# A fused graph-layer kernel: slot 5's one-hots moved behind block B's held sum, and block A transposed ahead of block B's second layer

## The chip, the cores and the metric

One core of one Trainium2 chip. The metric is the device time of one execution, in microseconds (us), and of several executions their median. Before the change it is 260.57 us (three runs, 260.36 to 260.77).

## What is computed

12500 nodes with 128 numbers each (`x`), 412500 edges with 48 numbers each (`edge_attr`), sorted by the node they point to (`dst`). The reference, cut to what matters:

```python
h = jnp.maximum(_layernorm(x, axis=-1), 0.0)
agg = jax.ops.segment_sum(edges, recv, num_segments=N_NODES)     # recv = dst
z = jnp.concatenate([h, agg, u], axis=1)      # u: the same 64 numbers for every node
out = x + (jax.nn.relu(z @ W1 + b1) @ W2 + b2)                   # hidden width 256
```

Everything is fp32. The edges are 79 MB of the 94 MB that are moved, the sum over edges most of the products.

## The kernel before, in words

**Staging.** The nodes are done in 12 turns of 1024; a turn has two blocks of 512, A (index 0) and B (index 1). The last 212 nodes (Z) come behind the loop. A turn's edges are 11 groups of 4 x 768 edges, kept in six slots: slots 0 to 3 and 5 hold two groups, slot 4 one. All tiles exist once; what overlaps is one turn's late part and the next one's early part.

**The sum over edges, as products.** For each slot VectorE compares an index with a row of numbers and so makes one-hots (`onehots`, tile `oh`, L745); TensorE multiplies edges by one-hots (`sums`, `su0` to `su5`, L801) into 28 sums per piece; ScalarE copies them to SBUF (`ss`, L805); a second product with one-hots of places (`pl`, made by VectorE at L751) adds them into two banks of 512 nodes, `ax` for A and `ay` for B (`place`, L823). What overlaps at the turn's ends goes through `pln` and `plf` (L785, `pc5`); the `pln` products read slot 5's copy.

**The nodes.** A and B are loaded from ScalarE's queue (`load_x`, L597), VectorE takes their statistics (`stats`, `stab`, L831) and from these `scab` and `shab`, ScalarE normalizes (`norm`, `xna` and `xnb`, L857), TensorE transposes (`turn`, `tu0` for A and `tu1` for B, L866), ScalarE copies the transposed blocks (`hta`, `htb`, L867). The first layer is two products per half of the hidden width, one from `hta` or `htb` (L876), one from the edge sums `ags` (L881); ScalarE applies bias and relu (L886). The second layer (`w20` for A, L907; for B `w21a`, 12 products at L901, and `w21`, 4 products at L907) is done in the next turn. VectorE adds its result to x + b2 in a held tile (`holda`, `holdb`, L911), and then overwrites `xba` or `xbb` by the next x + b2 (`add_b`, L861). When `xbb` is made, x of B is free and ScalarE issues the next load of B. All held tiles are stored at the end.

**What sets the order.** `body` lists the operations of a turn by hand, once for all engines. Each engine gets those of its own, in that order, as its queue; `Flow.order` works out the semaphores. An engine does its queue strictly in turn, so that a wait holds back all that stands behind it. VectorE, ScalarE, SP and GpSimd run a loop over the turns.

TensorE has a loop of its own (`Flow.run`): its turn is cut at an operation named by `f.mark`. What stands from there on (block "second") is placed at the loop's head, the rest ("first") behind it, so that a pass does the late part of one turn and the early part of the next. Operations named in `f.brief` are passed over in the first pass, where there is no second layer of an earlier turn: a compare on the register `turn` chooses between a block that only increments semaphores ("brief") and one that does the products ("whole"), and both come together in a block "both".

SP issues the loads of edges slot by slot as soon as TensorE has used them; the last in a turn is `le5.1`, slot 5's second group.

Of the kernel before, what the change touches and what calls it, by code (L numbers as in the profile page):

```python
# [28 lines left out]
R = 4  # L29
# [25 lines left out]
class Flow:  # L55
# [14 lines left out]
    def op(self, eng, name, reads, writes, emit, dma=False, late=None):  # L70
        self.seq.append(dict(eng=eng, name=name, r=tuple(reads), w=tuple(writes), emit=emit, dma=dma, it=self.at, late=late or {}))
# [119 lines left out]
    def run(self):  # L191
# [22 lines left out]
        def ahead(e, late=False):  # L214
            for n, c in sorted(self.ahead[e].items()):
                if (e == "PE" and n in self.weights) == late:
                    self.of[e].wait_ge(self.sem[n], (self.rank[n, c] + self.extra[n]) * self.unit(n))

        def repeat(o, i):
            waits = []  # L220
            for n, back in self.body.get(o["name"], []):
                u = self.unit(n)
                waits.append((n, self.sem[n], regs[(o["eng"], u, (self.at_lo[n] - lo - back + self.extra[n]) * u)]))
            self.emit(o, waits, i)
# [26 lines left out]
        pe = nc.tensor  # L251
        blocks = {}

        def part(name, over, come=True):

            if come:
                pe.br("pe_" + name)
            blocks[name] = nc.switch_bb("pe_" + name, parent=over and blocks[over])

        def either(under, yes, no):  # L260

            pe.br_lt(j, under, on_true="pe_" + yes, on_false="pe_" + no)

        n = 4
# [35 lines left out]
        at = "first"  # L300
        for brief, some in groupby(own[:cut], lambda o: o["name"] in self.brief):
            some = list(some)
            if not brief:
                for o in some:
                    if o["name"] in self.stops:
                        stop = "at_" + o["name"]
                        at = "go_" + o["name"]
                        above, under, to = over[stop]
                        part(stop, above)
                        either(under, to, at)  # L310
                        part(at, stop, False)
                    repeat(o, None)
                continue
            either(n + 1, "brief", "whole")
            part("brief", at, False)
            ahead("PE", True)
            for o in some:
                if o["name"] in self.sem:
                    pe.sem_inc(self.sem[o["name"]], 1)
            pe.br("pe_both")  # L320
            part("whole", at, False)
            for o in some:
                repeat(o, None)
            part("both", at)
        pe.br("pe_head")
        part("after", "gate2", False)
        self.straight(end)
# [151 lines left out]
def kernel(  # L479
# [37 lines left out]
    def bank(name):  # L517
        return psum.tile([P, BN], F32, name=name)
# [4 lines left out]
    ph = [bank("ph0"), bank("ph1")]  # L523
# [66 lines left out]
    f = Flow(nc, tc)  # L590
    op = f.op
    A, B, Z = 0, 1, 2

    def dma(eng, name, reads, writes, dst_ap, src_ap):
        def emit(i):
            with nc.allow_non_contiguous_dma(reason="small pieces"):
                return [f.of[eng].dma_start(dst_ap(i) if callable(dst_ap) else dst_ap, src_ap(i) if callable(src_ap) else src_ap)]  # L597
        op(eng, name, reads, writes, emit, dma=True)
# [31 lines left out]
    def rows_of(ap, i, a, m, r):  # L630
        return span(ap, i, a, m * r).rearrange("(p r) d -> p (r d)", r=r)

    def load_x(k, a, m=P, eng="ACT"):
        r = RR[k]
        dv = xt[k].rearrange("p r d -> p (r d)")
        q = m - m % 16
        dma(eng, f"lx{k}", [], [f"x{k}"], dv[:q], lambda i: rows_of(x, i, a, q, r))
        if q < m:
            dma(eng, f"lx{k}t", [], [f"x{k}t"], dv[q:m], lambda i: rows_of(x, i, lambda i: a(i) + q * r, m - q, r))
# [101 lines left out]
    def onehot(name, o, reads, r):  # L741

        k, n = r.shape[1], r.shape[2]
        ov = o.rearrange("p (k n) v -> p k n v", k=k)
        op("DVE", f"oh{name}", reads + ["iota_v"], [f"oh{name}"], lambda i: [nc.vector.tensor_tensor(  # L745
            ov, iota_v[:, None, None, :].to_broadcast([P, k, n, V]), r[:, :, :, None].to_broadcast([P, k, n, V]), OP.is_equal)])
# [6 lines left out]
    def onehots(s):  # L753
        g = SLOTS[s]
        onehot(s, oh[s], ["rel_i"], rel_i[:, g[0] - 1:g[0]] if len(g) == 1 else rel_i[:, g[0] - 1:g[1]:g[1] - g[0]])

    def split(name, o, some, reads, value):

        emits, c = [], 0
        for j, frm, w, _, _ in some:  # L760
            emits.append((c, j, frm, w))
            c += w
        op("DVE", name, reads + ["iota_w"], [name], lambda i: [
            nc.vector.tensor_scalar(o[:, c:c + w], iota_w[:, frm:frm + w], value(j), None, OP.is_equal) for c, j, frm, w in emits])
# [4 lines left out]
    def places_far():  # L769
        split("plf", plf, far_, ["off_i"], lambda j: off_i[:, SLOTS[-1][j] - 1:SLOTS[-1][j]])  # L770
# [17 lines left out]
    def keep_ends():  # L788
        op("ACT", "ssf", ["ss5"], ["ssf"], lambda i: [nc.scalar.copy(ssf, ss[5])])
# [17 lines left out]
    def sums(s):  # L807
        m = len(SLOTS[s])
        add_up(s, s % 2, oh[s], e[s], ss[s], [f"e{s}.{j}" for j in range(m)], m * CG, {1: (10, 36), 2: (36,)}.get(s, ()))
# [53 lines left out]
    def turn(k, m=P, bk=None, key="PT", eng="ACT"):  # L863
        pv = (pt if bk is None else bk)[:, :RR[k] * P].rearrange("p (r c) -> p r c", r=RR[k])
        copy = nc.scalar.copy if eng == "ACT" else nc.vector.tensor_copy
        op("PE", f"tu{k}", [f"xn{k}", "ident"], [key], lambda i: [nc.tensor.transpose(pv[:, r, :m], xn[k][:m, r], ident[:m, :m]) for r in range(RR[k])])  # L866
        op(eng, f"hT{k}", [key], [f"hT{k}"], lambda i: [copy(hT[k][:, :, :m], pv[:, :, :m])])  # L867

    def sums_out(k, m=P):
        h, r = HI * (k % 2), RR[k]  # L870
        op("ACT", f"ag{k}", [f"bk{k % 2}"], [f"ag{k}"], lambda i: [
            nc.scalar.copy(ag[k // 2][h:h + DE, :, :m], agg[k % 2][h:h + DE, :m * r].rearrange("p (c r) -> p r c", r=r))])
# [25 lines left out]
    def second_begun(k, bk, key, n):  # L898
        ov = bk.rearrange("p (r d) -> p r d", r=R)
        op("PE", f"w2{k}a", [f"hid{k}.{a}" for a in range(NH)] + ["w2"], [key], lambda i: [  # L900
            nc.tensor.matmul(ov[:, r], hid[k][:, a, r], w2[:, a], start=(a == 0), stop=(a == NH - 1)) for r in range(n) for a in range(NH)])  # L901
# [101 lines left out]
    def body(it):  # L1003
        f.at = it

        def add_slots(*some):
            for s in some:
                sums(s)
                if it < NIT - 1:
                    load_e(s, 1)  # L1010

        keep = lambda i: (i + NIT - 2) % (NIT - 1)
        add_slots(0, 1)
        stats(A)
        farthest()
        fetch(1)
        add_slots(2)
        stats(B)
        variance(0, (A, B))
        root(0)  # L1020
        onehots(0)
        add_slots(3)
        shift(0)
        norm(A, (0,))
        add_slots(4)
        norm(A, (1, 2))
        onehots(1)
        add_slots(5)
        norm(A, (3,))
        norm(B, range(R))  # L1030
        onehots(2)
        onehots(3)
        place(0, (0, 1))
        for s in (1, 2, 3, 4):
            place(s)
        place_ends((0, 1))
        second(A, P, ph[A], "PH0", keep)
        add_b(A)
        for s in (4, 5):
            onehots(s)  # L1040
        second_begun(B, ph[B], "PH1", R - 1)
        sums_out(A)
        sums_out(B)
        if it < NIT - 1:
            load_x(A, lambda i: (i + 1) % NIT * IN)
        turn(A)
        turn(B, P, po, "PO")
        second(B, P, ph[B], "PH1", keep, R - 1)
        add_b(B)
        keep_ends()  # L1050
        if it < NIT - 1:
            load_x(B, lambda i: (i + 1) % NIT * IN + BN)
        places_far()
        fetch_off(1)
        for s in (0, 1, 2, 3, 4):
            places(s)
        places_near()
        layers(layer_x)
        layers(layer_e)
        layers(relu)  # L1060
# [48 lines left out]
    for it in range(NIT):  # L1109
        body(it)  # L1110
# [1 line left out]
    f.at = NIT + 1  # L1112
    ends = [f"ot{k}" for k in range(3)] + [f"x{k}" for k in (A, B)] + [f"hold{k}.{j}" for k in (A, B) for j in range(NIT - 1)]
    op("SP", "end", [], ends, lambda i: [nc.sync.nop(nofuse=True)])
    f.mark, f.half, f.stops = "tu0", "of2", ("su1.b", "su1.c", "su2.b")
    f.brief, f.weights = ("w20", "w21a"), ("lw1h", "lw1a", "lw1b", "lw2")
    f.order((0, NIT - 1))
    tc.mark_branch_hint_location("skip", engines=[ET.PE, ET.DVE])
# [35 lines left out]
```

## Time and profile before

| | |
|---|---|
| median of 3 runs | 260.57 us (260.36 to 260.77) |
| the profiled execution | 260.67 us |
| its span, first to last instruction | 258.9 us |
| mean granted TensorE clock over the span | 0.965 |
| share of the span: TensorE, VectorE, ScalarE | 92%, 89%, 49% |
| moved by DMA | 94.33 MB, 364 GB/s over the span |
| longest waits of VectorE: for the load of B, 11 times | 6.9 us in sum, 0.8 at most |
| ScalarE's wait for A's transposes, 11 times | 12.2 us in sum, 2.1 at most |
| SP's wait for TensorE to free a slot, 11 times | 46.8 us in sum, 4.9 at most |

Times in the views are us from the start of the span, in one profiled execution. PE is TensorE, PEld its loading of weights, DVE VectorE, ACT ScalarE; `x4` counts instructions, and an fp32 product of the program is two of them. What stands in square brackets is the idle time of the engine ahead of the row and what ended it. A matmul's end is modelled, so that TensorE looks busy where it is not at its peak; a hole there is seen by the starts.

### The profile page before, as it was taken

The page shows a single profiled execution, that of the slowest core. Times are in us where ns is not written, and L with a number is a line of the kernel's source. Part 1 is how long each engine was busy: PE and PEld are TensorE (multiplying, and loading weights), DVE is VectorE, ACT ScalarE, POOL GpSimd, SP SyncE. Part 2 cuts the span into 40 slices and gives each one's busy share as a digit, 9 for nine tenths or more (in the row PEclk, how much of TensorE's full clock was granted, in tenths as well). Part 3 has the DMA queues.
Part 4 walks back from the last instruction along what each step waited for, and adds up shares of the span by engine and source line. Part 5 has one row for each costly group of instructions (what it writes and reads, how often), then busy time and mean ns, then how long its engine had stood idle before and what let it go on. Part 6 is the DMA issues. An engine that isn't in the chain of part 4 may idle for free.

```text
span 258.9 us, 17101 instructions
## 1 busy us (share of the span) xinstructions
PE 238.8 (92%) x7539; PEld 188.7 (73%) x7540; DVE 230.8 (89%) x572; ACT 127.9 (49%) x315; POOL 5.2 (2%) x18
## 2 busy tenths in 40 slices
PE   1866699899999999999999999999999999999990
PEld 1766565885976968949949869779589499598680
DVE  6699998978998998998998989989989989989740
ACT  5510273553644725725835646447257358355520
POOL 5000000000000000000000000000000000002000
PEclk9967579999999999999999999999999999999999
DMA  6999999999999999999999999999999999969951
GB/s 189 339 385 388 364 387 392 390 390 393 377 392 389 389 392 387 390 392 384 390 394 385 390 393 386 392 386 385 391 383 390 391 389 390 394 230 363 366 208 65
DMA packets 79508, 94.33 MB, mean 364 GB/s; under 512 B 3227, under 2 KB 72797, under 8 KB 79494
## 3 DMA queue, kind: packets, MB, share of 16 engines
q1 hardware_dynamic: 76086, 88.06, 95.5%
q10 hardware_dynamic: 3312, 6.03, 6.1%
q8 instruction: 7, 0.11, 0.2%
q0 software_dynamic: 96, 0.07, 0.1%
q14 instruction: 7, 0.06, 0.1%
HBM read 87.75 MB, written 6.40 MB: 364 GB/s over the span
## 4 chain that ended last, share of the span: by engine, by line
PE 78%; SPq 14%; DMA 4%; issue 1%; DVE 0%
PE s L801 23%; SPq L597 14%; PE ph L907 12%; PE ph L876 7%; PE ax L823 6%; PE ph L901 6%; PE pt L881 4%; PE pt L876 4%; DMA e<-in_edge_attr_dram 4%; PE ph L881 4%; PE po L876 4%; PE pt L866 2%; PE po L866 2%; PE ax L785 1%; PE ay L785 1%
## 5 line engine op out<-in xcount | busy, mean ns | idle before, releaser
L745 DVE TENSOR_TENSOR oh<-iota_v,rel_i 128x1344 f32<-128x1344 f32 (+1 forms) x78 | 108.7, 1435 | 0.0
L801 PEld LDWEIGHTS s<-e,oh 128*28 128x28 f32 x6336 | 74.2, 111 | 16.8 <-issue 14.5
L801 PE MATMUL s<-e,oh 128*28 128x48 f32 x6336 | 76.9, 212 | 7.4 <-issue 3.5
L886 ACT ACTIVATE hida<-pt,bias 128x512 f32<-128x512 f32 x12 | 8.2, 687 | 50.2 <-PE pt L881 50.2
L857 ACT ACTIVATE xna<-xa,shab,scab 128x128 f32<-128x128 f32 x48 | 23.7, 493 | 13.0 <-DVE shab L851 12.6
L805 ACT COPY ss<-s 128x96 f32<-128x96 f32 (+1 forms) x72 | 16.5, 229 | 26.5 <-PE s L801 25.7
L751 DVE TENSOR_SCALAR pl<-iota_w,off_i 128x186 f32<-128x186 f32 x117 | 27.6, 311 | 0.4
L907 PE MATMUL ph<-w,hida 128*128 128x128 f32 x192 | 24.6, 281 | 0.0
L857 ACT ACTIVATE xnb<-xb,shab,scab 128x128 f32<-128x128 f32 x48 | 23.5, 490 | 1.2
L907 PEld LDWEIGHTS ph<-w,hida 128*128 128x128 f32 x192 | 22.3, 191 | 0.6
L823 PE MATMUL ay<-pl,ss 128*48 128x186 f32 (+1 forms) x120 | 20.9, 324 | 0.0
L823 PE MATMUL ax<-pl,ss 128*48 128x186 f32 (+1 forms) x120 | 20.9, 324 | 0.0
L823 PEld LDWEIGHTS ax<-pl,ss 128*48 128x48 f32 x120 | 14.5, 129 | 4.1
L831 DVE BATCH_NORM_STATS2 stab<-xb 128x6 f32<-128x128 f32 x48 | 10.5, 282 | 6.9 <-DMA xb<-in_x_dram 6.9
L901 PE MATMUL ph<-w,hidb 128*128 128x128 f32 x132 | 16.5, 275 | 0.0
L901 PEld LDWEIGHTS ph<-w,hidb 128*128 128x128 f32 x132 | 15.6, 192 | 0.0
L823 PEld LDWEIGHTS ay<-pl,ss 128*48 128x48 f32 x120 | 14.5, 129 | 0.0
L876 PE MATMUL pt<-hta,w1h 128*128 128x512 f32 x24 | 13.5, 643 | 0.4 <-ACT hta L867 0.4
L881 PE MATMUL po<-ags,w1a 48*128 48x512 f32 x24 | 13.5, 641 | 0.0
L881 PE MATMUL pt<-ags,w1a 48*128 48x512 f32 x24 | 13.5, 641 | 0.0
L867 ACT COPY hta<-pt 128x512 f32<-128x512 f32 x12 | 7.0, 586 | 12.2 <-PE pt L866 12.2
L881 PE MATMUL ph<-ags,w1a 48*128 48x512 f32 x48 | 12.3, 589 | 0.0
(151 smaller groups left out, 330.3 us busy)
## 6 DMA issues: line engine op xcount, KB each, us to landing
e<-in_edge_attr_dram SPq DMA_DIRECT2D x133, 576.0 KB, 8.7
xa<-in_x_dram ACTq DMA_DIRECT2D x11, 256.0 KB, 5.4
xb<-in_x_dram ACTq DMA_DIRECT2D x11, 256.0 KB, 5.4
out_dram<-holda SPq DMA_DIRECT2D x11, 256.0 KB, 3.1
out_dram<-holdb SPq DMA_DIRECT2D x11, 256.0 KB, 3.1
holda<-in_dst_dram SPq DMA_DIRECT2D x4, 384.0 KB, 5.6
e<-in_edge_attr_dram SPq DMA_DIRECT2D x1, 720.0 KB, 4.7
xa<-in_x_dram SPq DMA_DIRECT2D x1, 256.0 KB, 6.6
```

What stands on the lines that cost most here:

```text
L597: return [f.of[eng].dma_start(dst_ap(i) if callable(dst_ap) else dst_ap, src_ap(i) if callable(src_ap) else src_ap)]
L745: op("DVE", f"oh{name}", reads + ["iota_v"], [f"oh{name}"], lambda i: [nc.vector.tensor_tensor(ov, iota_v[:, None, None, :].to_broadcast([ ...
L751: nc.vector.tensor_scalar(out[:, j], iota_w, o[j], None, OP.is_equal) for j in range(len(o))])
L801: nc.tensor.matmul(S[k][NV * c:NV * c + V, j * DE:(j + 1) * DE], o[:, (j * CG + c) * T + t], ev[:, j * CG + c, t * DE:(t + 1) * DE], start ...
L805: op("ACT", f"ss{name}", [f"S{k}"], [f"ss{name}"], lambda i: [nc.scalar.copy(sv.rearrange("p j d -> p (j d)"), S[k][:, :m * DE])])
L823: out.append(nc.tensor.matmul(agg[bk][h:h + DE, at:at + w], sv[:, j], pv[:, j, frm:frm + w], start=bk in fresh and bk not in seen, stop=Tr ...
L831: op("DVE", f"st{k}", [f"x{k}", f"x{k}t"], [f"st{k}"], lambda i: [nc.vector.bn_stats(st[k // 2][:m, c + r], xt[k][:m, r]) for r in range(R ...
L857: nc.scalar.activation(xn[k][:m, r], xt[k][:m, r], AF.Relu, bias=sh[n][:m, c + r:c + r + 1], scale=sc[n][:m, c + r:c + r + 1])])
L876: nc.tensor.matmul(o, w1h[:, a * P:(a + 1) * P], hT[k][:, :, :m], start=first, stop=False, skip_group_check=True)])
L881: nc.tensor.matmul(o, w1a[h:h + DE, a * P:(a + 1) * P], ag[k // 2][h:h + DE, :, :m], start=False, stop=True, skip_group_check=True)])
L901: nc.tensor.matmul(ov[:, r], hid[k][:, a, r], w2[:, a], start=(a == 0), stop=(a == NH - 1)) for r in range(n) for a in range(NH)])
L907: nc.tensor.matmul(ov[:m, r], hid[k][:, a, r, :m], w2[:, a], start=(a == 0), stop=(a == NH - 1)) for r in range(begun, RR[k]) for a in ran ...
```

## The change

Three things are moved in `body`. Slot 5's one-hots go from behind slot 4's to behind B's held sum and addition (`second(B, ...)`, `add_b(B)`, `keep_ends()`). Block A's transposes and their copy (`turn(A)`) go from behind the issue of A's load to ahead of it, and ahead of B's second layer (`second_begun`); the copies of the edge sums (`sums_out`) now stand ahead of both. To allow this, TensorE's turn is cut at `tu1` instead of `tu0`, and `w20` and `w21a`, which were one group with one choice between "brief" and "whole", become two groups with a choice each, since `tu0` stands between them.

```diff
@@ Flow.run
-            either(n + 1, "brief", "whole")
-            part("brief", at, False)
-            ahead("PE", True)
+            tag = some[0]["name"]
+            either(n + 1, "brief_" + tag, "whole_" + tag)
+            part("brief_" + tag, at, False)
+            if tag == self.brief[0]:
+                ahead("PE", True)
             for o in some:
                 if o["name"] in self.sem:
                     pe.sem_inc(self.sem[o["name"]], 1)
-            pe.br("pe_both")
-            part("whole", at, False)
+            pe.br("pe_both_" + tag)
+            part("whole_" + tag, at, False)
             for o in some:
                 repeat(o, None)
-            part("both", at)
+            part("both_" + tag, at)
+            at = "both_" + tag
@@ body
-        for s in (4, 5):
-            onehots(s)
-        second_begun(B, ph[B], "PH1", R - 1)
+        onehots(4)
         sums_out(A)
         sums_out(B)
+        turn(A)
+        second_begun(B, ph[B], "PH1", R - 1)
         if it < NIT - 1:
             load_x(A, lambda i: (i + 1) % NIT * IN)
-        turn(A)
         turn(B, P, po, "PO")
         second(B, P, ph[B], "PH1", keep, R - 1)
         add_b(B)
         keep_ends()
         if it < NIT - 1:
             load_x(B, lambda i: (i + 1) % NIT * IN + BN)
+        onehots(5)
         places_far()
@@ the names
-    f.mark, f.half, f.stops = "tu0", "of2", ("su1.b", "su1.c", "su2.b")
+    f.mark, f.half, f.stops = "tu1", "of2", ("su1.b", "su1.c", "su2.b")
```

VectorE's queue in the late part of a turn, before. `oh_91` and `oh_92` are the one-hots of slots 4 and 5, `holda` and `holdb` the held tiles, `plf` the first places of the next turn:

```order
L911 TENSOR_TENSOR holda<-ph_70,xba 128x512
L861 TENSOR_TENSOR xba<-xa,b_sb 128x512
L745 TENSOR_TENSOR oh_91<-iota_v,rel_i 128x672
L745 TENSOR_TENSOR oh_92<-iota_v,rel_i 128x1344
L911 REGISTER_ALU
L911 TENSOR_TENSOR holdb<-ph_71,xbb 128x512
L861 TENSOR_TENSOR xbb<-xb,b_sb 128x512
L764 TENSOR_SCALAR plf<-iota_w,off_i 128x46
```

And after (the lines are three higher in the changed file):

```order
L914 TENSOR_TENSOR holda<-ph_70,xba 128x512
L864 TENSOR_TENSOR xba<-xa,b_sb 128x512
L748 TENSOR_TENSOR oh_91<-iota_v,rel_i 128x672
L914 REGISTER_ALU
L914 TENSOR_TENSOR holdb<-ph_71,xbb 128x512
L864 TENSOR_TENSOR xbb<-xb,b_sb 128x512
L748 TENSOR_TENSOR oh_92<-iota_v,rel_i 128x1344
L767 TENSOR_SCALAR plf<-iota_w,off_i 128x46
```

`oh_92` has moved behind `holdb` and `xbb`; nothing else changes on VectorE.

TensorE's program at the end of the loop's body, before. `w20` is the row with `hida`, `w21a` the one with `hidb`; L262 and L320 are the compare and the end of "brief", L257 the jump behind "whole". A's transposes stand in the block at the loop's head, behind L269:

```order
L785 MATMUL ay<-pln,ss_106 48x46
L262 COMPARE_AND_BRANCH
L320 UNCONDITIONAL_BRANCH
L907 MATMUL ph_70<-w_141,hida 128x128 x8
L901 MATMUL ph_71<-w_141,hidb 128x128 x6
L257 UNCONDITIONAL_BRANCH
```

And after:

```order
L788 MATMUL ay<-pln,ss_106 48x46
L262 COMPARE_AND_BRANCH
L322 UNCONDITIONAL_BRANCH
L910 MATMUL ph_70<-w_141,hida 128x128 x8
L257 UNCONDITIONAL_BRANCH
L869 MATMUL pt<-ident,xna 128x128 x4
L262 COMPARE_AND_BRANCH
L322 UNCONDITIONAL_BRANCH
L904 MATMUL ph_71<-w_141,hidb 128x128 x6
L257 UNCONDITIONAL_BRANCH
```

A's transposes (`pt<-ident,xna`) stand between `w20` and `w21a`, with a jump and a compare more; the block at the loop's head begins with B's transposes (`po<-ident,xnb`). On ScalarE the copy of A (`hta<-pt`) stands behind the copies of the edge sums and ahead of the issue of A's load, where it stood behind it.

## The prediction

> **What bounds the kernel now.** I read the page first, for the share of each engine, then the table of stretches for one turn of the loop, then the chain of waits over all turns, then the timelines of VectorE, ScalarE and TensorE around the change, and last the landing times of the edge loads. The page's first part:
>
> ```profile
> PE 238.8 (92%) x7539; PEld 188.7 (73%) x7540; DVE 230.8 (89%) x572; ACT 127.9 (49%) x315; POOL 5.2 (2%) x18
> ```
>
> TensorE and VectorE are both nearly full, so the average does not decide. One turn in the table of stretches (PE, PEld, DVE, ACT, POOL, clock, DMA share, GB/s):
>
> ```profile
> 116.40:134.50 18.10, 18.10 (x614) 14.19 (x612) 17.17 (x43) 9.87 (x26) 0.00 (x0) 1.00 1.08 389
> ```
>
> TensorE looks full, VectorE has 0.9 us left, and the DMA engines move 389 GB/s at a share of 1.08: three candidates within a few per cent. The chain of waits (start, us, what) gives the pace. L907 hida x16 is block A's second layer, `w20`:
>
> ```profile
> 39.59 10.01 DMA e<-in_edge_attr_dram
> 49.65 0.71 PE s L801 x48
> 52.24 1.98 PE ph L907 x16
> ...
> 70.39 1.98 PE ph L907 x16
> ...
> 129.18 0.99 PE pt L876 x2
> 130.17 0.86 PE po L876 x2
> ...
> 232.90 1.98 PE ph L907 x16
> ...
> 237.54 0.92 PE pt L876 x2
> ```
>
> From 70.39 to 232.90 are nine turns: 162.51 / 9 = 18.06 us each. At 49.60 the kernel is held by an edge load, the last of its turn (`le5.1`, slot 5's second group); `w20` follows 2.64 us later. The same load one turn later and in the last turn, by SP's timeline and its time to landing:
>
> ```profile
> 57.70 1.35 SPq L597 DMA_DIRECT2D e<-in_edge_attr_dram  x1
> ```
>
> ```profile
> DMA to landing us min/median/max: 9.8/9.8/9.8
> ```
>
> ```profile
> 219.07 1.35 SPq L597 DMA_DIRECT2D e<-in_edge_attr_dram  x1
> ```
>
> ```profile
> DMA to landing us min/median/max: 10.0/10.0/10.0
> ```
>
> Landings at 67.50 and 229.07: 161.57 / 9 = 17.95 us a turn. The loads run 0.11 us a turn faster than the compute; from landing to `w20` it is 2.64, then 2.89, and 3.83 us in the last turn. So the DMA is not what sets 18.06, but it is only 0.11 us below. What does set it, on VectorE:
>
> ```profile
> 107.04 1.55 DVE L745 TENSOR_TENSOR oh<-iota_v,rel_i 128x1344 f32<-128x1344 f32 x1
> 108.51 0.68 DVE L911 TENSOR_TENSOR holda<-ph,xba 128x512 f32 x1
> 109.23 0.69 DVE L861 TENSOR_TENSOR xba<-xa,b_sb 128x512 f32<-128x512 f32 x1
> 109.84 2.32 DVE L745 TENSOR_TENSOR oh<-iota_v,rel_i 128x672 f32<-128x672 f32 x2
> 112.08 0.68 DVE L911 TENSOR_TENSOR holdb<-ph,xbb 128x512 f32 x1
> 112.80 0.69 DVE L861 TENSOR_TENSOR xbb<-xb,b_sb 128x512 f32<-128x512 f32 x1
> ...
> 116.48 0.87 DVE L831 BATCH_NORM_STATS2 stab<-xa 128x6 f32<-128x128 f32 x4
> ...
> 118.90 0.29 DVE L831 BATCH_NORM_STATS2 stab<-xb 128x6 f32<-128x128 f32 x1 [0.62 <-DMA xb<-in_x_dram]
> ```
>
> ScalarE issues block B's load once `xbb` is done (rows of ScalarE's timeline, and the load's time to landing):
>
> ```profile
> 109.95 0.41 ACTq L597 DMA_DIRECT2D xa<-in_x_dram  x1
> 110.40 0.59 ACT L867 COPY hta<-pt 128x512 f32<-128x512 f32 x1 [1.08 <-PE pt L866]
> ...
> 113.52 0.34 ACTq L597 DMA_DIRECT2D xb<-in_x_dram  x1
> ```
>
> ```profile
> DMA to landing us min/median/max: 5.4/5.4/5.4
> ```
>
> This is a closed ring: `xbb` ends at 113.49, the load of B is issued at 113.52 and lands 5.4 us later, `stab<-xb` starts at 118.90, VectorE then has no other wait until the next `xbb`. Period: 113.49 - 100.83 (the last turn's 118.90 - 18.07) = 12.66 of VectorE, plus 5.4, is 18.06, exactly the pace. The only idle time of VectorE in a turn, 0.62 us, lies in this ring. TensorE hangs on it through `shab` and ScalarE's queue:
>
> ```profile
> 122.29 0.49 ACT L857 ACTIVATE xna<-xa,shab,scab 128x128 f32<-128x128 f32 x1 [1.05 <-DVE shab L851]
> ...
> 122.82 1.02 ACT L857 ACTIVATE xna<-xa,shab,scab 128x128 f32<-128x128 f32 x2
> 123.74 0.22 ACT L805 COPY ss<-s 128x96 f32<-128x96 f32 x1
> ```
>
> ```profile
> 123.82 0.24 PE L823 MATMUL ax<-pl,ss 128*48 128x93 f32 x1
> 123.83 0.24 PE L823 MATMUL ay<-pl,ss 128*48 128x93 f32 x1
> 123.90 0.28 PE L785 MATMUL ax<-plf,ssf 128*48 128x140 f32 x1
> 124.02 0.32 PE L785 MATMUL ay<-pln,ss 128*48 128x140 f32 x1
> ```
>
> Until 123.83 the products for `ax` and `ay` start 0.01 us apart; the first `pln` product comes 0.12 us after its partner, just after slot 5's copy ends (123.96). That is the wait that slows TensorE, hidden in a column that says 18.10 of 18.10.
>
> **The change part by part.** Call E the end of B's second layer. By TensorE's timeline
>
> ```profile
> 110.07 0.60 PE L866 MATMUL po<-ident,xnb 128*128 128x128 f32 x4
> 110.50 0.61 PE L907 MATMUL ph<-w,hidb 128*128 128x128 f32 x4
> ```
>
> E is 111.11, and `holdb` could start there. VectorE takes up a product 0.04 us after it ends: in the last stage `w20` starts at 245.16, lasts 1.98, and `ota` starts at 247.18.
>
> ```profile
> 245.16 1.98 PE ph L907 x16
> ```
>
> ```profile
> 247.18 0.69 DVE L909 TENSOR_TENSOR ota<-ph,xba 128x512 f32<-128x512 f32 x1 [2.06 <-PE ph L907]
> ```
>
> *Slot 5's one-hots moved.* Now `holdb` waits in the queue behind them until 112.08. Afterwards it starts at 111.15 (0.93 earlier), with VectorE idle from about 110.7. `xbb` ends at 112.56 instead of 113.49, B's load is issued at about 112.6 and lands at 118.0. The one-hots follow; they take 1.47 us (start 107.04 to the next start, 108.51; neighbours overlap by 0.08). VectorE reaches `stab<-xb` at 118.90 - 0.93 + 1.47 - 0.70 = 118.74, where 0.70 is the wait that goes (0.62 and the overlap of 0.08). The load has been there for 0.7 us, so the ring through the DMA opens (its length falls to about 18.06 - 1.47 = 16.6) and the wait moves to `holdb`. What is late next is the longer ring E, `holdb`, `xbb`, one-hots, `stab`, `shab`, `xna`, slot 5's copy, `pln`, `w20` ... E: 0.16 us shorter, 17.90 us. VectorE's own work, 18.06 - 0.70 = 17.36, fits into it. Slot 5's one-hots are not needed before the next turn's slot 5 (its products wait for `le5.1`, which lands at 67.50 + 3 x 17.95 = 121.35 in this turn), so ending 2 us later, at about 114, costs nothing; with that cover gone TensorE would wait for all of it.
>
> Then 17.90 meets the loads' 17.95, and the loads are the bound. The lead of 3.83 us in the last turn can fall to what the held turns show, 2.89 (with the copy's wait) or 2.64 (without): a gain of 0.94 to 1.19 us, and I take the middle, 1.07, close to (18.06 - 17.95) x 10 turns.
>
> *The transposes of A moved.* Four fp32 transposes, nothing added: they stand ahead of 12 products instead of behind them. `hta` then is copied behind the two copies of sums and ahead of the issue of A's load. Now the order is: `xba` ends at 109.92, the issue takes 109.95 to 110.36, only then `hta` (110.40 to 110.99), and the first layer's pair for A takes 0.99 us where that for B takes 0.86: 0.13 us of waiting. This goes. But it lies behind E, and TensorE's next appointment is `pln`, where it waits for slot 5's copy anyway: the 0.13 us only lengthens that wait. Worth 0 per turn, and 0.92 - 0.86 = 0.06 in the last one, behind which nothing waits. `htb` is next to be late: it starts when B's transposes end (110.07 + 0.60, E - 0.44), takes as long as `hta`, 0.59, and is done at E + 0.15 to 0.2; TensorE then has A's pair of 0.86 under way and wants its weights during the second of the two; I estimate up to 0.1 us to spare, and if it is late the same `pln` wait takes it up. A's load is now behind `hta` in ScalarE's queue: at worst, with `hta` starting only when `xba` ends, it is issued 0.59 later, at 110.54, and lands at 115.9, still ahead of `stab<-xa` at 116.48. Nobody else waits for it.
>
> *B's load 0.9 us earlier.* It is 256 KB, 0.67 us at 389 GB/s, taken from edge loads that land between 118.0 and 118.9. `le5.1`, the one that binds, lands after both (121.35) and has the same bytes ahead of it: cost 0 for the sum, and no more than 0.1 a turn if the interleaving is uneven. The Trainium skill says in DMA: Bandwidth & Descriptors, section Issuing engines are not separate DMA queues, that loads started by different engines share the same 16 DMA engines and interleave; by that rule an earlier load of B can gain nothing from the loads' side, and the 389 GB/s at a full share, in a turn with loads of both engines, agrees.
>
> *TensorE's control flow.* One jump and one compare more per turn:
>
> ```profile
> L257 PEldq COMPARE_BRANCH  x11: 177/177/177, 53.4 to 234.1; - x11
> ```
>
> ```profile
> L262 PEldq COMPARE_BRANCH  x106: 67/71/442, 2.1 to 239.9; - x106
> ```
>
> 0.177 + 0.071 = 0.25 us of TensorE's sequencer, at most 0.62 with the longest compare. Today's jump (L257) stands behind `w20` and the 12 products of `w21a`, and the first of them falls at 53.4, while `w20` runs from 52.24 to 54.22: the sequencer is then more than 0.8 us ahead of the products. I take 0 for the new one.
>
> Sum: 1.07 + 0.06 = 1.13. The profiled execution took 260.67 us (span 258.9, 1.8 around it); it becomes 259.5, and the median of the runs, 260.57, becomes 259.4.
>
> **The rivals.**
> *The loads do not hold it.* If the loads, asked for earlier, also land faster than 17.95, the ring of 17.90 decides: 0.16 x 11 + 0.06 = 1.8, so 258.8. Against it: the share of the DMA engines is full in every turn.
> *The wait only changes its place.* The 0.16 is what is left of 0.93, 1.47 and 0.70. If `holdb`, now woken by TensorE, and the work behind it lose 0.1 to 0.2 us (0.04 for waking and 0.08 of overlap are measured, for one place each), or the waits on `xna` or `htb` take it, 0 to 0.05 a turn remains: 260.0 to 260.6.
> *The new jump drains TensorE.* It stands in E's own ring, ahead of `w21a`. If the sequencer is not ahead there, 0.25 to 0.62 us a turn are added to 17.90; from 0.16 on it is a loss. With 0.3: 18.20, 0.14 x 11 = 1.5 slower, 262.1. Against it: TensorE's products run on across the jump that is there, and the page's row of instruction fetches is small for eleven turns:
>
> ```profile
> q8 instruction: 7, 0.11, 0.2%
> ```
>
> The Trainium skill, Runtime: NRT & Kernel Launch, section Instruction fetch mechanics, has a rule that speaks against the change: a taken branch whose target is outside the fetched window stalls until the page is fetched. By that rule the new jump could cost a fetch each turn; the row above shows 7 fetches in all, so the jumps of today's loop do not do it.
> That the change does not do what it says is no rival here: the order of the instructions shows both moves.
>
> **How the numbers follow.** A measurement of this kernel can tell about 0.2%, 0.52 us, from no change. Forecast (259.4; 259.1 to 259.9 by itself): 0.58. Loads faster too: 0.12. Wait in another place: 0.22. Jump: 0.08. Faster than 260.05 are the first two and a little of the third, less some of the first: 0.69; same 0.23; slower 0.08. The range holds the first three cases, 258.8 to 260.6.
>
> **What would show it.** In the profile of the changed kernel: no wait of `stab<-xb` for the DMA, instead one of `holdb` for TensorE of 0.3 to 0.6 us; no wait of `pt` for `hta`; `w20` from turn to turn in 17.95 us and `le5.1` again just ahead of its products; the loads' own pace unchanged. Wrong it would be with a pace of 18.0 or more, with the wait at `pln` as long as now, or with holes in TensorE between A's transposes and B's second layer.

## The result and the profile after

The changed kernel takes 259.28 us (median of 12 runs, 258.44 to 260.02); beside it the kernel before took 260.69 us (12 runs, 260.01 to 261.37). The ratio is 0.9948, with a 95% interval of 0.9937 to 0.9959: faster by about half a per cent, with the whole interval below 1. The profiled execution took 259.39 us (span 257.5), against 260.67 (span 258.9) before. TensorE's granted clock was lower in the first 50 us (0.79 before and 0.86 after, between 26 and 50 us), but 1.00 from 50 to 233 us in both executions, so that the turns can be compared. Lines behind the changed part of `Flow.run` stand three further down than before: block A's and B's second layer is L910 now, `holda` and `holdb` L914, the x statistics L834.

The page's first part of the changed kernel, and one turn in its table of stretches (same columns as before):

```profile
PE 238.0 (92%) x7539; PEld 187.6 (73%) x7540; DVE 231.3 (90%) x572; ACT 129.1 (50%) x315; POOL 4.5 (2%) x18
```

```profile
116.00:133.94 17.94, 17.94 (x623) 14.04 (x624) 17.16 (x43) 9.88 (x25) 0.00 (x0) 1.00 1.08 390
```

Nothing in these rows tells the change: the same engines are full to the same tenths. The chain of waits does (start, us, what):

```profile
70.06 1.98 PE ph L910 x16
...
228.97 0.71 PE s L804 x48
...
231.56 1.98 PE ph L910 x16
...
236.21 0.86 PE pt L879 x2
```

`w20` goes from 70.06 to 231.56 in nine turns, 161.50 / 9 = 17.944 us each, where it was 18.06. Slot 5's second group (L804 x48) starts at 228.97. Its load, `le5.1`, by SP's timeline and the time to landing:

```profile
218.93 1.34 SPq L600 DMA_DIRECT2D e<-in_edge_attr_dram  x1
```

```profile
DMA to landing us min/median/max: 10.0/10.0/10.0
```

It lands at 228.93, 0.04 us before its products start. (The time to landing is given in tenths, so a landing read this way is good to 0.05 us.) In the trace it is so in every turn of the loop from 49.53 on; before the change the lead grew from 0.04 to about 1.1 us over the turns. So the loads now hold each turn, and from landing to `w20` it is 231.56 - 228.93 = 2.63 us. VectorE around the change, by its timeline:

```profile
110.64 0.69 DVE L914 TENSOR_TENSOR holdb<-ph,xbb 128x512 f32 x1 [0.47 <-PE ph L910]
111.37 0.69 DVE L864 TENSOR_TENSOR xbb<-xb,b_sb 128x512 f32<-128x512 f32 x1
111.98 1.55 DVE L748 TENSOR_TENSOR oh<-iota_v,rel_i 128x1344 f32<-128x1344 f32 x1
...
118.22 0.87 DVE L834 BATCH_NORM_STATS2 stab<-xb 128x6 f32<-128x128 f32 x4
```

The bracket has moved: `stab<-xb` waits for nothing, and VectorE is idle for 0.47 us ahead of `holdb`, until B's second layer ends at E. ScalarE's timeline shows its part of it:

```profile
108.80 0.59 ACT L870 COPY hta<-pt 128x512 f32<-128x512 f32 x1
109.43 0.34 ACTq L600 DMA_DIRECT2D xa<-in_x_dram  x1
110.19 0.59 ACT L870 COPY htb<-po 128x512 f32<-128x512 f32 x1 [0.81 <-PE po L869]
...
112.09 0.34 ACTq L600 DMA_DIRECT2D xb<-in_x_dram  x1
```

`hta` is copied ahead of A's load now. B's load goes out at 112.09 and lands 5.3 us later, at 117.4, which is 0.8 us before `stab<-xb` wants it. TensorE at the products of slot 5's ends:

```profile
110.00 0.61 PE L910 MATMUL ph<-w,hidb 128*128 128x128 f32 x4
```

```profile
123.40 0.28 PE L788 MATMUL ax<-plf,ssf 128*48 128x140 f32 x1
123.41 0.28 PE L788 MATMUL ay<-pln,ss 128*48 128x140 f32 x1
```

E is 110.61. The first `pln` product comes 0.01 us after its partner, where 0.12 lay between them: the wait for slot 5's copy is gone. Two rows of the table of waits between 70 and 245 us (us in total, times, longest) sum it up:

```profile
DVE holdb L914 <- PE ph L910: 4.5, 10, 0.5
...
PEld s L804 <- DMA e<-in_edge_attr_dram: 0.5, 3, 0.2
```

The table counts only three waits for the edge load, of 0.2 us at most; the landings show it in every turn.

### The profile page after: what moved, and what is told of

Its sections match the earlier page's. It is cut to its first block, busy times and chain, and to the rows that moved or that the text cites. A ratio compares the mean times of both kernels' runs of the same rounds, so it can differ in the third digit from the quotient of the medians.

```text
span 257.5 us, 17114 instructions
## 1 busy us (share of the span) xinstructions
PE 238.0 (92%) x7539; PEld 187.6 (73%) x7540; DVE 231.3 (90%) x572; ACT 129.1 (50%) x315; POOL 4.5 (2%) x18
## 4 chain that ended last, share of the span: by engine, by line
PE 88%; DVE 4%; DMA 3%; issue 1%; ACT 1%; SPq 0%; ACTq 0%; DVEq 0%
PE s L804 27%; PE ph L910 12%; PE ph L879 8%; PE ax L826 7%; PE ph L904 6%; PE pt L884 5%; PE pt L879 4%; PE ph L884 4%; PE po L879 4%; DMA holda<-in_dst_dram 3%; PE po L869 2%; PE pt L869 2%; PE ax L788 2%; DVE oh L748 1%; DVE pl L754 1%
## 5 line engine op out<-in xcount | busy, mean ns | idle before, releaser
L804 PEld LDWEIGHTS s<-e,oh 128*28 128x28 f32 x6336 | 73.3, 109 | 16.5 <-issue 12.0
L804 PE MATMUL s<-e,oh 128*28 128x48 f32 x6336 | 77.0, 210 | 6.1 <-issue 2.5
L910 PE MATMUL ph<-w,hida 128*128 128x128 f32 x192 | 24.6, 281 | 0.0
L910 PEld LDWEIGHTS ph<-w,hida 128*128 128x128 f32 x192 | 22.3, 191 | 0.6
L914 DVE TENSOR_TENSOR holdb<-ph,xbb 128x512 f32 x12 | 8.3, 692 | 5.6 <-PE ph L910 5.6
L879 PE MATMUL pt<-hta,w1h 128*128 128x512 f32 x24 | 12.4, 598 | 0.2 <-ACT hta L870 0.2
L879 PE MATMUL ph<-hta,w1h 128*128 128x512 f32 x24 | 12.3, 592 | 0.0
```

What stands on the lines that cost most here:

```text
L804: nc.tensor.matmul(S[k][NV * c:NV * c + V, j * DE:(j + 1) * DE], o[:, (j * CG + c) * T + t], ev[:, j * CG + c, t * DE:(t + 1) * DE], start ...
L879: nc.tensor.matmul(o, w1h[:, a * P:(a + 1) * P], hT[k][:, :, :m], start=first, stop=False, skip_group_check=True)])
L910: nc.tensor.matmul(ov[:m, r], hid[k][:, a, r, :m], w2[:, a], start=(a == 0), stop=(a == NH - 1)) for r in range(begun, RR[k]) for a in ran ...
L914: op("DVE", f"ho{k}", [key, f"xb{k}"] + (["spare"] if k == A else []), [f"hold{k}.{keep(f.at)}"], lambda i: [nc.vector.tensor_tensor(cols( ...
```

## The experiments

The theory under test has three bounds: the ring through B's load (18.06 us before the change), the longer ring from E through `holdb`, `stab<-xb` and slot 5's copy back to E (17.90), and the loads (17.95). The rival: the transposes, or VectorE's busy time, or the loads alone explain the gain. The first four versions stand beside one set of runs of the kernel before (median 260.61 us, 18 runs), the last four beside another (260.77 us, 30 runs); each version ran 4 to 12 times. A ratio is to the kernel before.

**Slot 5's one-hots alone.** In the kernel before:

```
-        for s in (4, 5):
-            onehots(s)
+        onehots(4)
         second_begun(B, ph[B], "PH1", R - 1)
...
             load_x(B, lambda i: (i + 1) % NIT * IN + BN)
+        onehots(5)
```

> The kernel before with slot 5's one-hots alone moved behind B's held sum and addition; A's transposes stay where they were. Theory of the ring (the pace before is VectorE's work plus the 5.4 us of B's load): the ring is open, the edge loads hold the pace, 17.94 us a turn; ScalarE still issues A's load ahead of A's copy, so the first layer still waits 0.13 us for it, but the waits for the last edge load swallow that. 259.3 to 259.4, as the changed kernel or 0.06 more. Rival (the first layer's wait for A's copy sets the pace, or both parts are needed): 260.0 to 260.7, pace 18.0 or more.

Measured: 259.13 us, ratio 0.9946 (0.9927 to 0.9965), 0.2 us below what was expected. From its chain:

```profile
69.87 1.98 PE ph L907 x16
...
128.33 0.98 PE pt L876 x2
...
231.37 1.98 PE ph L907 x16
```

The pace is 161.50 / 9 = 17.944, that of the whole change, though `hta` is still late: block A's pair of products takes 0.98 us where it takes 0.86 in the changed kernel. Within the intervals, this half is the whole gain.

**A's transposes alone.** In the changed kernel, slot 5's one-hots go back:

```
-        onehots(4)
+        for s in (4, 5):
+            onehots(s)
         sums_out(A)
...
             load_x(B, lambda i: (i + 1) % NIT * IN + BN)
-        onehots(5)
```

> The changed kernel with slot 5's one-hots put back ahead of B's held sum; A's transposes stay ahead of B's second layer. Theory of the ring: the ring is closed as before, pace 18.06, B's statistics wait 0.6 us a turn for B's load; the first layer no longer waits for A's copy, and the wait at the pln products grows by the same 0.1 to 0.2 us. 260.6, at most 0.1 less than before. Rival (the first layer's wait counts): 0.13 x 11 = 1.4 less, 259.2.

Measured: 260.65 us, ratio 1.0000 (0.9988 to 1.0012). Chain and waits:

```profile
69.52 1.98 PE ph L910 x16
...
232.05 1.98 PE ph L910 x16
```

```profile
DVE stab L834 <- DMA xb<-in_x_dram: 5.5, 9, 0.7
...
PEld ay L788 <- ACT ss L808: 0.9, 5, 0.2
```

The pace is 162.53 / 9 = 18.06, as before the change. The wait of the first layer for `hta` is gone (A's pair takes 0.86 us) and comes back at `pln`, where TensorE now is named as waiting for slot 5's copy: the first `pln` product of a turn comes 0.27 us after its partner (122.92 to 123.19), where it was 0.12. That is what the prediction meant by a wait that is swallowed.

**Slot 5's one-hots between `holdb` and `xbb`.** In the changed kernel:

```
         second(B, P, ph[B], "PH1", keep, R - 1)
+        onehots(5)
         add_b(B)
...
-        onehots(5)
         places_far()
```

> The changed kernel with slot 5's one-hots between B's held sum and B's addition: holdb starts as early as in the changed kernel, xbb as late as before. Theory of the ring (it runs through xbb and the load of B): closed as before, pace 18.06, 260.6. Rival (what counts is that holdb itself comes earlier and frees the bank of B's second layer for the first layer): 259.3, as the changed kernel.

Measured: 264.34 us, ratio 1.0137 (1.0117 to 1.0157). Both expectations fell: it is slower than either kernel. Its chain, and VectorE in one turn:

```profile
71.00 1.98 PE ph L910 x16
...
236.59 1.98 PE ph L910 x16
```

```profile
112.55 0.69 DVE L914 TENSOR_TENSOR holdb<-ph,xbb 128x512 f32 x1 [0.46 <-PE ph L910]
113.15 1.55 DVE L748 TENSOR_TENSOR oh<-iota_v,rel_i 128x1344 f32<-128x1344 f32 x1
114.62 0.68 DVE L864 TENSOR_TENSOR xbb<-xb,b_sb 128x512 f32<-128x512 f32 x1
...
120.59 0.87 DVE L834 BATCH_NORM_STATS2 stab<-xb 128x6 f32<-128x128 f32 x4 [0.50 <-DMA xb<-in_x_dram]
```

The pace is 165.59 / 9 = 18.40. The expectation worked with two separate rings and took the ring through B's load to be as long as before, since the same work stands on VectorE. But `holdb` can't start before E, so VectorE idles 0.46 us there, and the one-hots then push `xbb`, and with it B's load, later after E than ever. Both waits now lie one behind the other in one ring: E, `holdb`, one-hots, `xbb`, load, `stab<-xb`, and on to E. So the length to watch is the time from the start of `holdb` to `stab<-xb` where `holdb` is woken by E: 8.04 us here, 7.58 in the changed kernel (118.22 - 110.64).

**Fewer bytes in the changed kernel.** The edge load that binds brings half of its bytes; half of that group's edges keep old values.

```
-        e[s][:, k * CG:(k + 1) * CG]
+        e[s][:, k * CG:(k + 1) * CG - less]
...
-        load_e(s, 1)
+        load_e(s, 1, cut=2 if s == 5 else 0)
```

> The changed kernel, with the last edge load of every turn (le5.1) bringing 288 KB instead of 576: half of that group keeps old edges, so the sums are of other edges; all products are still done. 288 KB are 0.74 us at 390 GB/s, so that the loads could run at 17.2 us a turn. Theory (after the change the loads are the bound at 17.94, and the next bound is the ring E, holdb, one-hots, stab, shab, slot 5's copy, pln at 17.90): pace 17.88 to 17.92, the wait at the pln products is back, 0.1 to 0.2 us a turn, no wait for edge loads in the late turns; 258.2 to 258.7. Rival (the loads are not the bound): pace 17.94 as in the changed kernel, 259.0 to 259.3.

Measured: 258.39 us, ratio 0.9926 (0.9902 to 0.9950). Its chain, and TensorE at the first `pln` product:

```profile
51.49 1.98 PE ph L911 x16
69.40 1.98 PE ph L911 x16
...
230.59 1.98 PE ph L911 x16
```

```profile
122.47 0.40 PE L789 MATMUL ax<-plf,ssf 128*48 128x140 f32 x2
122.61 0.32 PE L789 MATMUL ay<-pln,ss 128*48 128x140 f32 x1
```

The pace falls to 161.19 / 9 = 17.910, no more: the wait before `pln` is back (0.14 us) and the ring of 17.90 has taken over. The loads do bind the changed kernel, by 0.03 us a turn. That is 0.3 us in all; the rest of the 0.9 us between the two medians doesn't come from the pace, and the intervals of the two ratios overlap.

**Fewer bytes in the kernel before.** The same edit there.

> The kernel before, but the edge load that binds after the change (slot 5's second group) brings 288 KB instead of 576 in the loop; half of that group's edges keep their old values. If the ring on VectorE through B's load sets the pace of the kernel before, the turns stay at 18.03 to 18.06 us and only the first turns, in which TensorE waits for that load, get shorter: 259.9 to 260.6. If the kernel before were bound by its loads, its turns would fall to 17.9 as they did with the same cut after the change, and the time to 258.4 to 259.0.

Measured: 259.57 us, ratio 0.9948 (0.9925 to 0.9971). Chain and waits of its profiled execution, which itself took 260.58:

```profile
70.56 1.98 PE ph L908 x16
...
232.82 1.98 PE ph L908 x16
```

```profile
DVE stab L832 <- DMA xb<-in_x_dram: 5.1, 9, 0.6
```

The pace is 162.26 / 9 = 18.03, and `stab<-xb` still waits in all nine turns. The same cut that brings the changed kernel to 17.91 leaves this one at 18.03, so its loads were not what set it. The total was below what I had expected (259.9 to 260.6). Only some 0.3 us of the 1.2 are pace. The rest may lie in the first turn of the loop, where TensorE's loading of weights waits for that load in the profile of the kernel before. From its table of waits between 40 and 52 us:

```profile
PEld s L801 <- DMA e<-in_edge_attr_dram: 0.8, 1, 0.8
```

With the load cut, the trace has no such wait. But that execution took 1.0 us more than the median of its runs and doesn't show the gain, and executions differ in the first turn by as much: the first `w20` comes at 52.13 in the changed kernel, at 51.49 with its load cut, and at 51.45 with full loads in the version with eight compares below. That part stays open. So the total of a run with a cut load doesn't tell what binds the turns: it fell by 1.2 us here, where the loads don't set the pace, and by 0.9 where they do. The pace tells it.

**Eight more compares on TensorE's sequencer.** In the changed kernel, between A's transposes and the 12 products:

```
+            base = at
+            if tag != self.brief[0]:
+                for q in range(8):
+                    either(1000 + q, f"hop{q}", "whole_" + tag)
+                    part(f"hop{q}", at, False)
+                    at = f"hop{q}"
             either(n + 1, "brief_" + tag, "whole_" + tag)
```

> The changed kernel with eight more compares on TensorE's sequencer in every turn, between A's transposes and the 12 products of B's second layer: 8 x 0.071 = 0.57 us of sequencer time at the very place of the jump that the change adds. If the sequencer runs that far ahead of the products there, as the prediction took it, the time stays at 259.1 to 259.5 and the 12 products start behind the transposes as now. If the jump drains TensorE, up to 0.57 us a turn are added to the ring of 17.90: a pace of up to 18.47 and 262 to 264.6.

Measured: 259.33 us, ratio 0.9946 (0.9923 to 0.9968), the pace by its chain unchanged at 161.45 / 9 = 17.94:

```profile
69.42 1.98 PE ph L916 x16
...
230.87 1.98 PE ph L916 x16
```

The compares of one turn, from 104 to 107.5 us, and the weight loads of the transposes and of the products behind them:

```profile
L262 PEldq COMPARE_BRANCH  x10: 68/68/218, 104.7 to 106.6; - x10
```

```profile
106.98 0.47 PEld L875 LDWEIGHTS pt<-ident,xna 128*128 128x128 f32 x4
107.42 1.20 PEld L910 LDWEIGHTS ph<-w,hidb 128*128 128x128 f32 x10
```

Eight of them fill the sequencer from 105.55 to 106.57 in the trace, 1.02 us and not the 0.57 I had put (each lasts 0.068, but they follow each other every 0.128). Even so they are through before the transposes' weights are loaded, and the 12 products follow with no hole. So the sequencer has 1 us to give at this place, and the jump rival is refuted.

**An extra operation ahead of `holdb`.** In the changed kernel, half of slot 4's one-hots once more (the same values):

```
         onehots(4)
+        again()
         sums_out(A)
```

> The changed kernel with one more operation on VectorE in every turn: half of slot 4's one-hots once more (128x336, about half of 0.77 us, so 0.37 to 0.42), ahead of holdb, where VectorE now idles 0.47 us waiting for the end of B's second layer. If the ring E, holdb, xbb, one-hots, stab is what is next to the loads, the extra lies in that idle time: pace 17.94 to 17.96, 259.1 to 259.6, holdb's wait down to 0.05 to 0.15 us. If VectorE's busy time is what counts, 0.4 a turn: pace 18.3, 263.

Measured: 259.33 us, ratio 0.9946 (0.9924 to 0.9968). VectorE's timeline:

```profile
110.20 0.51 DVE L761 TENSOR_TENSOR oh<-iota_v,rel_i 128x336 f32<-128x336 f32 x1
110.64 0.69 DVE L919 TENSOR_TENSOR holdb<-ph,xbb 128x512 f32 x1
```

The operation costs nothing: `holdb` starts at 110.64, to the hundredth where it started without it. Of the wait of 0.05 to 0.15 us that was expected to be left ahead of `holdb`, the row shows none.

**The same operation behind `xbb`.**

```
+        again()
         onehots(5)
         places_far()
```

> The same extra operation (128x336, 0.37 to 0.42 us a turn) placed behind xbb, just ahead of slot 5's one-hots. If the ring E, holdb, xbb, one-hots, stab, shab, xna, slot 5's copy, w20, E is 17.90 us long, it becomes 18.27 to 18.32 and sets the pace: 262.4 to 263.0, although VectorE still idles 0.4 to 0.5 us at holdb. If VectorE has its 0.47 us to spare wherever the work stands, the time stays at 259.1 to 259.6.

Measured: 263.08 us, ratio 1.0087 (1.0061 to 1.0114): 3.8 us above the changed kernel, for the operation that cost nothing ahead of `holdb`. Chain, VectorE and one row of the table of waits between 70 and 245 us:

```profile
70.04 1.98 PE ph L915 x16
...
234.98 1.98 PE ph L915 x16
```

```profile
111.38 0.69 DVE L919 TENSOR_TENSOR holdb<-ph,xbb 128x512 f32 x1 [0.46 <-PE ph L915]
...
112.72 0.50 DVE L761 TENSOR_TENSOR oh<-iota_v,rel_i 128x336 f32<-128x336 f32 x1
...
119.39 0.86 DVE L839 BATCH_NORM_STATS2 stab<-xb 128x6 f32<-128x128 f32 x4
```

```profile
PEld ay L793 <- ACT ss L813: 2.6, 9, 0.3
```

The operation takes 0.42 us to the next start, and the pace is 164.94 / 9 = 18.33 = 17.91 + 0.42. (Pace and time come out just above the ranges expected.) VectorE idles 0.46 us at `holdb` as before and can't use it, since the ring runs through the work behind it; where it comes back to TensorE, at `pln`, TensorE waits for slot 5's copy in nine turns.

One rule now holds these paces together. Take 17.91 (the changed kernel with its loads out of the way) and add what the way from `holdb` to `stab<-xb` is longer than 7.58:

| kernel | way, us | 17.91 + excess | measured pace |
|---|---|---|---|
| before (from E + 0.04 = 111.15 to 118.90) | 7.75 | 18.08 | 18.06 |
| one-hots between `holdb` and `xbb` | 8.04 | 18.37 | 18.40 |
| extra operation behind `xbb` | 8.01 | 18.34 | 18.33 |
| changed kernel | 7.58 | 17.91, loads 17.94 | 17.94 |

The rule was made after the runs, with 17.91 from the cut loads and 7.58 from the changed kernel; the first three rows are its test. What it tests is that the rest of the circle, from `stab<-xb` back to E, is as long in all of them; in the first row `holdb` isn't woken by E, and the row says only that TensorE follows VectorE at that distance. The ways are those of one turn each, and in the version with the one-hots between they vary by 0.1 us from turn to turn.

## Why the prediction was right

*The ring through B's load.* Right. Undoing the move of the one-hots alone brings back 18.06 and the wait of `stab<-xb`; making it alone gives 17.944.

*`holdb` at E + 0.04, the way 0.16 us shorter, a ring of 17.90.* Right in size: the way fell from 7.75 to 7.58, and the ring shows itself at 17.91 once the last load is cut. The idle time forecast for `holdb` (from about 110.7 to 111.15, so some 0.45) came as 0.47.

*The loads are the bound at 17.95.* Right: 17.944, with `le5.1` landing 0.04 us before its products in every turn. They bind by 0.03 us a turn, where 0.05 was forecast.

*The gain of 0.94 to 1.19 us, of which I took 1.07.* This term was mis-sized, by 0.27. By the last `w20` the profiled execution gained 232.90 - 231.56 = 1.34. Of this 1.20 is the lead, 3.83 down to 2.63: the end of the range without the wait for slot 5's copy, since TensorE, held at `le5.1` in every turn, finds that copy done. I had put the middle and not chosen between the two cases; the runs show the first `pln` product 0.01 us behind its partner wherever the loads hold the turn, and 0.14 behind it once the load is cut. The other 0.14 is `le5.1` landing at 228.93 instead of 229.07; what made it is not shown, and in the profiled execution with only the one-hots moved the last `w20` came 0.19 us earlier still.

*A's transposes, 0 a turn and 0.06 in the last.* Right: the move alone gave a ratio of 1.0000, the last pair takes 0.86 instead of 0.92, and the 0.13 us came back in front of `pln`. `htb` ended at 110.78, E + 0.17, inside the 0.15 to 0.2 forecast.

*B's load earlier, at no cost.* Right: it is issued 0.93 us earlier after E (1.48 instead of 2.41), and the loads' pace is 17.944 against 17.952, the same within the tenths in which landings are given.

*One jump and one compare more, at 0.* The price of 0 was right, the reading of what is added wrong. The trace of the changed kernel has these rows, the last from 104 to 107.5 us alone:

```profile
L257 PEldq COMPARE_BRANCH  x11: 177/177/177, 53.7 to 233.2; - x11
```

```profile
L262 PEldq COMPARE_BRANCH  x118: 67/71/1342, 2.1 to 237.7; - x118
```

```profile
L262 PEldq COMPARE_BRANCH  x2: 215/216/218, 105.4 to 106.2; - x2
```

There are 12 compares more than before (118 instead of 106), but the same 11 jumps, although the program's order lists one more. And the compare that is added in a turn lasts 0.215 us, not the 0.071 of the middle one; the one of 1.342 us stands at 7.5 us, ahead of the loop. Nor is anything more fetched: the rows of the two instruction queues are the same in both profiles, 7 packets on q8, which the prediction counted, and 7 on q14, which it left out.

*The sum.* 1.13 was forecast. The profiled execution gained 1.28 (260.67 to 259.39), its span 1.4, and the medians of the runs side by side 1.41 (260.69 to 259.28). So the forecast was short by some 0.3 us, all of it in the first term; that 259.4 for the median came so close to 259.28 is in part luck, since the kernel before took 260.69 in these runs and not the 260.57 it was worked out from.

*The rivals.* That the loads don't hold is shown wrong by the landings and by the pace, which fell from 17.944 to 17.910 when the load was cut; the gain in total is no proof. That the wait only changes its place was true of the place and wrong of the price: the idle time moved to `holdb`, where an operation put into it cost nothing. That the jump drains TensorE is shown wrong by the changed kernel itself, whose 12 products follow the transposes with no hole (in its chain, 54.11 + 0.44 to 54.55), and by the eight compares.

## What to carry to other kernels

When engines wait for each other in a circle, follow the wait round until it comes back to its start, and measure each part of the circle from the event that can't come earlier; an operation's price is then set by whether it stands inside that stretch or in front of it, and not by how busy its engine is. Before work is moved behind a wait, check what it pushes that others start from: here the issue of a load, which made the version between `holdb` and `xbb` the worst of all. And once a circle opens, the gain ends at the next bound, so measure that bound's own pace (here the landings of one load, turn by turn) before you forecast a size.

## What the runs showed of the hardware

Compares on TensorE's sequencer that stood in a row lasted 0.068 us each but followed one another only every 0.128 us; even 1.02 us of them cost nothing at this place. VectorE's one-hots of 128x336 took 0.42 us to the next start, those of 128x1344 1.47. Four of the small do the work of the large one in 1.68, so I estimate that (1.68 - 1.47) / 3 = 0.07 us of each operation is a fixed price.
